# A graph layer's end list written anew, with its sums in another PSUM bank and the first rows' normalization cut into parts

## The chip, the cores and the metric

The kernel runs on one core of a Trainium2 chip. The metric is device microseconds of one execution. Several executions are timed and their median is taken; one more execution is taken with the hardware profiler, and all rows shown here are from that one.

## The reference

A graph layer with 12,500 nodes of 128 features and 200,000 edges, sorted by destination. What is computed, cut to what matters:

```python
h = maximum(layernorm(x), 0)                       # N x 128
score = ((h @ W_Q.T)[dst] * (h @ W_K.T)[src]).sum(-1) / sqrt(128) * exp(-edge_weight)
# of each node the 16 best edges are kept; softmax over them
alpha = w / denom[dst]
agg = segment_sum(alpha[:, None] * (h[src] @ W_msg.T), dst)
out = x + relu(h @ W_self.T + agg)
```

## The kernel before, in words

The edges stand in 1,563 chunks of 128. Fourteen chunks make a group: 112 groups, numbered 0 to 111. The last one, called L in the code, has 9 chunks. A group owns the nodes whose edges begin in it, and it reads one chunk of the next group too, so it works on 15 chunks.

For each chunk GpSimd gathers 128 rows of normalized features from the table `h_tab` in HBM with one indirect DMA (`let_go` and `gather`, L176). VectorE copies the indices first (`ix`, L191). The rows of a group lie in a tile `hs`; there are eight such buffers, so the rows of group 8 go where those of group 0 lay. Groups 0 to 3 (`RAW`) are gathered before the table exists: their raw rows come from the input `x`, and are normalized in place, by one ScalarE activation for each chunk (`normed`, L221). Groups 0 and 1 are normalized in the preparation. Groups 2 and 3 are begun in window 0 (`raw_begun`, one chunk) and finished at the end of windows 1 and 2 (`raw_finished`, 13 chunks in one block).

The work on one group is a pipeline of small stages, each a few instructions:

- `far_of`, `to_edges`, `edges_turned`, `away`, `places`: TensorE and ScalarE build one-hot matrices of which edge belongs to which node and slot. All their matmuls write the one PSUM bank named `a`, and ScalarE empties it.
- `q_to_edges` (L589) spreads the query to edges, in blocks of four chunks; `scores` (L598, VectorE) multiplies it with the gathered rows, one instruction a chunk; `scores_in_slots` (L606).
- `slots_by_node` (L614), `slots_out` (L619, ScalarE), `node_by_slots` (L622): scores are put in 40 slots for each node. These use the PSUM bank `e`.
- `best` (L628 to L640, VectorE): reads bank `e`, finds the 16 best; `sum_of_exps` (L645, ScalarE).
- `kept_to_edges` (L657) brings the marks back to edges, in the bank `x`; `one_over_sum`, `on_edges` (L650 to L670, VectorE), `exps` (L674, ScalarE), `weights` (L678 and L679, VectorE, into `alz`).
- `sums` (L687): 15 accumulating matmuls of weights and rows, each in two passes, into columns 384 to 511 of bank `e`; `sums_out` (L692, ScalarE).
- `sums_turned` (L695), `sums_turned_out` (L699, ScalarE), `products` (L702 and L703), `output` (L707, VectorE), `store`: all in the bank `s`. The last four groups are stored by an indirect DMA of GpSimd (L716).

The instruction order is written by hand. The loop over `i` from -3 to 110 is a window: in it group `i` is scored, group `i-1` is put in slots, `i-2` gets its best, `i-3` its weights and sums, `i-4` its output, while `i+1` and `i+2` are prepared. Each engine executes its part of this list in order. Instructions of different engines on one PSUM bank wait for each other, whichever columns they use. After the loop a second list, written out call by call, brings groups L-5 to L to their ends: this is the end list. One small check of the inputs (`later`, L452 to L470) is executed by VectorE at the end of each early window.

Of the kernel before, what the change touches and what calls it, by code (L numbers as in the profile page):

```python
# [14 lines left out]
AF = mybir.ActivationFunctionType  # L15
OP = mybir.AluOpType
# [4 lines left out]
P = 128  # L21
# [29 lines left out]
PRE = 16  # L51
STEP = 8
WW = STEP * (NJ - 1) + WN
# [23 lines left out]
def gnn_layer(  # L77
# [27 lines left out]
    nc = tc.nc  # L105
# [26 lines left out]
    def bank(tag, bufs):  # L132
        return psum.tile([P, 512], F32, tag=tag, bufs=bufs, name=tag)
# [81 lines left out]
    def normed(rows, n0, n1, rs, sm):  # L215

        if n0 == 0:
            nc.vector.reciprocal(rs, rs)
            nc.vector.scalar_tensor_tensor(sm, sm, -0.5, rs, op0=OP.mult, op1=OP.mult)
        for t in range(n0, n1):  # L220
            nc.scalar.activation(rows[:, t, :], rows[:, t, :], AF.Relu, bias=sm[:, t:t + 1],  # L221
                                 scale=rs[:, t:t + 1])
# [9 lines left out]
    def raw_begun(g):  # L232
        normed(T[g]["hs"], 0, 1, *T[g]["raw"])

    def raw_finished(g):
        normed(T[g]["hs"], 1, own[g], *T[g]["raw"])

    w0 = rows_pool.tile([P, NJ], F32, name="w0")
    zpad = rows_pool.tile([P, D], F32, name="zpad")
# [15 lines left out]
    with tc.tile_pool(name="edges", bufs=1) as ep, ExitStack() as stage:  # L255
# [38 lines left out]
        xs, t = [], 0  # L294
# [208 lines left out]
    with tc.tile_pool(name="win", bufs=2) as win:  # L503
# [79 lines left out]
        def q_to_edges(g, b):  # L583
            j0, j1 = 4 * b, min(4 * b + 4, chunks[g])
            if j0 >= j1:
                return
            T[g]["pq", b] = pq = bank("q", 3)
            for j in range(j0, j1):
                nc.tensor.matmul(pq[:, (j - j0) * P:(j - j0 + 1) * P],  # L589
                                 lhsT=T[g]["to_e"][:, j * P:(j + 1) * P], rhs=T[g]["q"], start=True, stop=True)  # L590

        def scores(g, b):
            if b == 0:
                T[g]["s"] = win.tile([P, NJ], F32, name="s", bufs=4)
            for j in range(4 * b, min(4 * b + 4, chunks[g])):
                c = GC * g + j
                prod = win.tile([P, D], F32, name="prod")
                nc.vector.scalar_tensor_tensor(  # L598
                    prod, rows_of(g, j), dec_all[:, c:c + 1],
                    T[g]["pq", b][:, (j % 4) * P:(j % 4 + 1) * P],  # L600
                    op0=OP.mult, op1=OP.mult, accum_out=T[g]["s"][:, j:j + 1])
# [15 lines left out]
        def slots_out(g):  # L617
            T[g]["eT"] = win.tile([KM + 1, P], F32, name="eT")
            nc.scalar.copy(T[g]["eT"], et[0:KM + 1, PRE:PRE + P])  # L619

        def node_by_slots(g):
            nc.tensor.transpose(et[:, 256:256 + KM + 1], T[g]["eT"], ident[0:KM + 1, 0:KM + 1])  # L622
# [31 lines left out]
        def kept_to_edges(g):  # L654
            T[g]["px"] = px = psum.tile([P, NJ + 1, 64], F32, tag="x", bufs=1, name="x")
            for j in range(chunks[g]):
                nc.tensor.matmul(px[:, j, 0:KM + 3], lhsT=upper(T[g]["to_e"][:, j * P:(j + 1) * P]),  # L657
                                 rhs=upper(T[g]["km"]), start=True, stop=True)
# [17 lines left out]
        def weights(g):  # L676
            n, kept = chunks[g], T[g]["kept"]
            nc.vector.tensor_tensor(kept[:, 0:n], T[g]["up"][:, 0:n], kept[:, 0:n], op=OP.mult)  # L678
            nc.vector.tensor_tensor(alz[g % 2].rearrange("e (j w) -> e j w", w=WW + STEP)[:, 0:n, 0:WN],  # L679
                                    T[g]["ow"][:, 0:n, :], bc(kept[:, 0:n], WN), op=OP.mult)  # L680


        def sums(g, part):
            n = chunks[g]
            half = n // 2
            for j in range(half) if part == 0 else range(half, n):
                nc.tensor.matmul(et[:, 384:384 + P], lhsT=alz[g % 2][:, WW * j + PRE:WW * j + PRE + P],  # L687
                                 rhs=rows_of(g, j), start=(j == 0), stop=(j == n - 1))

        def sums_out(g):  # L690
            T[g]["agn"] = win.tile([P, D], F32, name="agn")
            nc.scalar.activation(T[g]["agn"], et[:, 384:384 + P], AF.Copy, scale=T[g]["rden"])  # L692

        def sums_turned(g):
            nc.tensor.transpose(so[:, 2 * P:3 * P], T[g]["agn"], ident)  # L695
# [24 lines left out]
        def at(g, stage, *args):  # L720
            if 0 <= g < G:
                stage(g, *args)


        for i in range(-3, G - 1):
            at(i + 3, load_nodes)
            if i == 8:
                nc.sync.dma_start(h_tab[N:N + P, :], zpad)
                nc.sync.dma_start(x_end[XT:XT + P, :], zpad)
                nc.sync.dma_start(x_end[0:XT, :], x[N - XT:N, :])  # L730
            def more(k):

                if i in (-1, 0, 1):
                    g = i + 6
                else:
                    g, k = (i + 4, k + 2) if k < 5 else (i + 5, k - 5)
                    if g < 8:
                        return
                if i >= -1 and g < G:
                    let_go(g, k)  # L740

            at(i, q_to_edges, 0)
            at(i - 5, output)
            at(i - 5, store)
            at(i - 3, weights)
            more(0)
            at(i - 4, sums_turned)
            at(i + 1, far_of, 0)
            at(i - 4, sums_turned_out)
            at(i + 1, q_out)  # L750
            at(i, q_to_edges, 1)
            at(i + 1, far_of, 1)
            for b in range(3):
                at(i - 1, slots_by_node, b)
            at(i + 1, far_of, 2)
            more(1)
            at(i - 2, best)
            more(2)
            at(i - 2, sum_of_exps)
            at(i - 1, slots_out)  # L760
            at(i, q_to_edges, 2)
            at(i + 1, far_of, 3)
            at(i + 2, h_turned)
            at(i, scores, 0)
            more(3)
            at(i + 1, to_edges)
            at(i + 2, h_turned_out)
            at(i - 2, kept_to_edges)
            at(i - 1, node_by_slots)
            at(i + 1, edges_turned)  # L770
            at(i - 3, sums, 0)
            at(i, scores, 1)
            more(4)
            at(i + 1, away, 0)
            at(i, q_to_edges, 3)
            at(i - 2, one_over_sum)
            at(i + 1, away, 1)
            at(i - 3, sums, 1)
            at(i, scores, 2)
            at(i - 2, on_edges)  # L780
            more(5)
            at(i + 1, away, 2)
            at(i - 3, sums_out)
            at(i - 4, products)
            at(i - 2, exps)
            at(i + 1, places)
            at(i, scores, 3)
            at(i, scores_in_slots)
            if i == 0:
                raw_stats(2)  # L790
                raw_stats(3)
                raw_begun(2)
                raw_begun(3)
            if i in (1, 2):
                raw_finished(i + 1)
            more(6)
            at(i + 2, q_made)
            if i > 0 and later:
                later.pop(0)()
# [5 lines left out]
        def turned(g):  # L805
            sums_turned(g)
            sums_turned_out(g)

        def all_sums(g):
            sums(g, 0)  # L810
            sums(g, 1)
            sums_out(g)

        def to_rows(g):
            products(g)
            output(g)
            store(g)

        def all_slots(g):
            for b in range(3):  # L820
                slots_by_node(g, b)

        def to_nodes(g):
            all_slots(g)
            slots_out(g)
            node_by_slots(g)

        def kept_on_edges(g):
            one_over_sum(g)
            on_edges(g)  # L830
            exps(g)
# [4 lines left out]
        weights(L - 3)  # L836
        turned(L - 4)
        all_slots(L - 1)
        slots_out(L - 1)
        best(L - 2)  # L840
        sum_of_exps(L - 2)
        q_to_edges(L, 1)
        node_by_slots(L - 1)
        to_rows(L - 4)
        all_sums(L - 3)
        kept_to_edges(L - 2)
        best(L - 1)
        sum_of_exps(L - 1)
        scores(L, 0)
        kept_on_edges(L - 2)  # L850
        turned(L - 3)
        kept_to_edges(L - 1)
        scores(L, 1)
        weights(L - 2)
        all_sums(L - 2)
        to_rows(L - 3)
        for b in range(2, blocks):
            q_to_edges(L, b)
            scores(L, b)
        scores_in_slots(L)  # L860
        to_nodes(L)
        kept_on_edges(L - 1)
        turned(L - 2)
        best(L)
        sum_of_exps(L)
        weights(L - 1)
        kept_to_edges(L)
        all_sums(L - 1)
        to_rows(L - 2)
        kept_on_edges(L)  # L870
        turned(L - 1)
        weights(L)
        all_sums(L)
        to_rows(L - 1)
        turned(L)
# [184 lines left out]
```

## Time and profile before

| | us |
|---|---|
| timed executions | 2051.35, 2051.93, 2052.34 |
| median | 2051.93 |
| profiled execution, its time | 2049.57 |
| profiled execution, its span | 2047.8 |
| gathers, 1507 of them, mean | 0.955 |
| start of the last gather of rows | 1995.29 |
| end of the last `output` (L707) | 2033.39 |

The span runs from the first to the last recorded instruction; 1.77 us of the time lie outside it. TensorE's share of busy time is 77%, GpSimd's 74%, VectorE's 63% and ScalarE's 50%, as averages over stages that have different limits.

### The profile page before, as it was taken

The numbers are of one execution on the slowest core, as the hardware profiler recorded it, in microseconds if no ns is written. First come the engines' busy times: TensorE is split into PE (matmuls) and PEld (weight loads), VectorE is DVE, ScalarE is ACT, GpSimd is POOL, SyncE is SP. The second block draws the span as 40 slices with busy tenths as digits, with TensorE's granted clock in tenths as the row PEclk, the third lists the DMA queues.
The fourth block names the chain that finished last, engine by engine and source line by source line (L and its number), as shares of the span: only waits on it lengthen the run. The fifth ranks groups of instructions, "written<-read, shape, count | busy, mean of one in ns | idle before, by whom it ended". The sixth has DMA issues, their size and how long they took to land. (4 is left out here: it accounts for less than half of the span.)

```text
span 2047.8 us, 42217 instructions
## 1 busy us (share of the span) xinstructions
PE 1581.4 (77%) x13800; PEld 1304.9 (64%) x13801; DVE 1281.2 (63%) x7001; ACT 1026.3 (50%) x2198; POOL 1508.7 (74%) x1580
## 2 busy tenths in 40 slices
PE   0368899987787878878888778787888888777784
PEld 0257777766666666666666666666666666666663
DVE  7567877766666666666666666566666666666553
ACT  6666566544444444444444445444444445444440
POOL 6777777777777777777777777777777777777770
PEclk9969999998998999999899999899999989989887
DMA  9521222222222222222222222222222222222220
GB/s 246 154 57 52 76 68 68 66 65 65 66 64 65 65 66 66 63 64 66 66 65 65 65 65 66 65 66 65 64 63 65 65 65 66 66 65 66 63 59 7
DMA packets 101472, 143.46 MB, mean 70 GB/s; under 512 B 31063, under 2 KB 74327, under 8 KB 100480
## 3 DMA queue, kind: packets, MB, share of 16 engines
q0 software_dynamic: 50144, 102.74, 19.2%
q1 hardware_dynamic: 51102, 37.99, 6.7%
q8 instruction: 108, 1.77, 0.4%
q14 instruction: 118, 0.97, 0.2%
HBM read 126.79 MB, written 14.40 MB: 69 GB/s over the span
## 5 line engine op out<-in xcount | busy, mean ns | idle before, releaser
L176 POOL DMA_INDIRECT hs<-h_tab,ix x1507 | 1439.9, 955 | 464.9 <-issue 303.5
L598 DVE SCALAR_TENSOR_TENSOR prod<-hs,dec_all,q 128x128 f32<-128x128 f32 x1674 | 508.0, 343 | 298.2 <-DMA hs<-h_tab,ix 260.0
L551 ACT ACTIVATE far<-a,minus 128x512 bf16<-128x512 f32 (+1 forms) x447 | 294.5, 659 | 534.9 <-PE a L549 527.7
L589 PE MATMUL q<-q,to_e 128*128 128x128 f32 x3348 | 515.3, 301 | 0.0
L589 PEld LDWEIGHTS q<-q,to_e 128*128 128x128 f32 x3348 | 484.7, 214 | 34.1 <-DVE prod L598 13.5
L687 PE MATMUL e<-hs,alz 128*128 128x128 f32 x3348 | 436.7, 284 | 4.6 <-DVE alz L679 4.6
L687 PEld LDWEIGHTS e<-hs,alz 128*128 128x128 f32 x3348 | 394.9, 193 | 32.0 <-issue 19.2
L574 ACT ACTIVATE aw<-a 128x400 bf16<-128x400 f32 x336 | 169.4, 504 | 312.7 <-PE a L572 312.7
L628 DVE TENSOR_SCALAR ell<-slots,e 128x40 f32<-128x40 f32 x112 | 28.4, 254 | 369.8 <-PE e L614 319.0
L695 PE MATMUL s<-ident,agn 128*128 128x128 f32 x112 | 38.2, 341 | 266.6 <-DVE kept L678 265.4
L549 PE MATMUL a<-rel,ident 112*128 112x512 bf16 (+1 forms) x447 | 196.1, 439 | 14.8 <-ACT far L551 14.8
L556 ACT ACTIVATE to_e<-far 128x1920 f32<-128x1920 bf16 x112 | 201.4, 1799 | 3.5
L695 PEld LDWEIGHTS s<-ident,agn 128*128 128x128 f32 x112 | 16.9, 151 | 282.7 <-issue 280.4
L614 PE MATMUL e<-opo,sl 128*41 128x40 f32 x3348 | 189.8, 230 | 0.9 <-DVE rden L650 0.9
L614 PEld LDWEIGHTS e<-opo,sl 128*41 128x41 f32 x3348 | 176.1, 144 | 13.2 <-DVE sl L606 1.0
L598 DVE DVE_READ_ACCUMULATOR prod<-hs,dec_all,q 128x1 f32 x1674 | 136.8, 82 | 0.0
L578 ACT ACTIVATE opo<-aw 128x1200 f32<-128x1200 bf16 x112 | 134.2, 1199 | 0.1
L191 DVE COPY ix<-idx_all 128x2 int32<-128x2 int32 x754 | 132.8, 191 | 0.0
L572 PE MATMUL a<-minus_at,pdT 32*128 32x400 bf16 x336 | 115.0, 342 | 18.0 <-ACT pdT L565 7.6
L657 PE MATMUL x<-km,to_e 128*128 128x43 bf16 x1674 | 61.4, 184 | 70.9 <-DVE km L640 66.0
L657 PEld LDWEIGHTS <-to_e 128*128 128x128 bf16 x1674 | 50.1, 97 | 102.3 <-DVE km L640 96.8
L606 DVE TENSOR_TENSOR sl<-opo,s 128x600 f32<-128x600 f32 x112 | 87.5, 782 | 3.9
(174 smaller groups left out, 1646.5 us busy)
## 6 DMA issues: line engine op xcount, KB each, us to landing
hs<-h_tab,ix POOLq DMA_INDIRECT x1507
h_r<-h_tab SPq DMA_DIRECT2D x112, 64.0 KB
x_t<-in_x_dram SPq DMA_DIRECT2D x108, 64.0 KB
out_dram<-o SPq DMA_DIRECT2D x108, 64.0 KB
xg<-in_x_dram SPq DMA_DIRECT2D x2, 1400.0 KB
h_tab<-xg SPq DMA_DIRECT2D x2, 1400.0 KB
xg<-in_x_dram SPq DMA_DIRECT2D x1, 1120.0 KB
h_tab<-xg SPq DMA_DIRECT2D x1, 1120.0 KB
```

What stands on the lines that cost most here:

```text
L176: nc.gpsimd.indirect_dma_start(out=T[g]["hs"][:, j, :], out_offset=None, in_=table[0:N, :], in_offset=bass.IndirectOffsetOnAxis(ap=index(j ...
L191: nc.vector.tensor_copy(ix[:, j0:j1], idx_all[:, GC * g + j0:GC * g + j1])
L549: nc.tensor.matmul(pr[:, 0:n1 - n0], lhsT=upper(ident[0:RR, g:g + 1]).to_broadcast([RR, P]), rhs=rel[:, n0:n1], start=True, stop=True)
L551: nc.scalar.activation(T[g]["far"][:, n0:n1], pr[:, 0:n1 - n0], AF.Square, bias=minus)
L556: nc.scalar.activation(T[g]["to_e"][:, 0:n], T[g]["far"][:, 0:n], AF.Relu, bias=1.0, scale=-1.0)
L572: nc.tensor.matmul(pr[:, 0:400], lhsT=T[g]["pdT"], rhs=minus_at.rearrange("k w j s -> k (w j s)")[:, n0:n1], start=True, stop=True)
L574: nc.scalar.activation(T[g]["aw"][:, n0:n1], pr[:, 0:400], AF.Square)
L578: nc.scalar.activation(T[g]["opo"].rearrange("e w j s -> e (w j s)"), T[g]["aw"], AF.Relu, bias=1.0, scale=-1.0)
L589: nc.tensor.matmul(pq[:, (j - j0) * P:(j - j0 + 1) * P], lhsT=T[g]["to_e"][:, j * P:(j + 1) * P], rhs=T[g]["q"], start=True, stop=True)
L598: nc.vector.scalar_tensor_tensor(prod, rows_of(g, j), dec_all[:, c:c + 1], T[g]["pq", b][:, (j % 4) * P:(j % 4 + 1) * P], op0=OP.mult, op1 ...
L614: nc.tensor.matmul(et[0:KM + 1, STEP * j:STEP * j + WN], lhsT=sl1[g % 2][:, j, :], rhs=T[g]["ow"][:, j, :], start=False, stop=(j == n - 1))
L687: nc.tensor.matmul(et[:, 384:384 + P], lhsT=alz[g % 2][:, WW * j + PRE:WW * j + PRE + P], rhs=rows_of(g, j), start=(j == 0), stop=(j == n ...
```

## The change

Three things are done. In the end list, the order of the calls is new, and all calls of `sums` write the bank `a` in place of bank `e` (inside the loop they stay in `e`). The normalization of the raw rows of groups 2 and 3 is no longer one block of 13 activations at the end of windows 1 and 2: three parts of three chunks go to ScalarE at three places in the same windows, and the last four chunks go to VectorE, as two `tensor_scalar` instructions each, where the block was.

```diff
-    def raw_finished(g):
-        normed(T[g]["hs"], 1, own[g], *T[g]["raw"])
+    def raw_finished(g, part):
+        rows, (rs, sm) = T[g]["hs"], T[g]["raw"]
+        if part < 3:
+            normed(rows, 1 + 3 * part, 4 + 3 * part, rs, sm)
+            return
+        for t in range(10, own[g]):
+            nc.vector.tensor_scalar(rows[:, t, :], rows[:, t, :], rs[:, t:t + 1], sm[:, t:t + 1],
+                                    op0=OP.mult, op1=OP.add)
+            nc.vector.tensor_scalar(rows[:, t, :], rows[:, t, :], 0.0, None, op0=OP.max)
...
-        def sums(g, part):
+        def sums(g, part, at=None):
             n = chunks[g]
+            if part == 0:
+                T[g]["pa"] = et[:, 384:384 + P] if at is None else at
             half = n // 2
             for j in range(half) if part == 0 else range(half, n):
-                nc.tensor.matmul(et[:, 384:384 + P], lhsT=alz[g % 2][:, WW * j + PRE:WW * j + PRE + P],
+                nc.tensor.matmul(T[g]["pa"], lhsT=alz[g % 2][:, WW * j + PRE:WW * j + PRE + P],
                                  rhs=rows_of(g, j), start=(j == 0), stop=(j == n - 1))
...
-            nc.scalar.activation(T[g]["agn"], et[:, 384:384 + P], AF.Copy, scale=T[g]["rden"])
+            nc.scalar.activation(T[g]["agn"], T[g]["pa"], AF.Copy, scale=T[g]["rden"])
...
+            def raw(part):
+                if i in (1, 2):
+                    raw_finished(i + 1, part)
...
             at(i + 1, far_of, 1)
+            raw(0)
             for b in range(3):
                 at(i - 1, slots_by_node, b)
...
             at(i - 1, slots_out)
+            raw(1)
             at(i, q_to_edges, 2)
             at(i + 1, far_of, 3)
+            raw(2)
             at(i + 2, h_turned)
...
             if i in (1, 2):
-                raw_finished(i + 1)
+                raw_finished(i + 1, 3)
...
         def all_sums(g):
-            sums(g, 0)
+            sums(g, 0, bank("a", 1)[:, 0:P])
             sums(g, 1)
             sums_out(g)
```

The two end lists side by side, from the first line in which they differ. `all_slots` holds `slots_out` now; `blocks` is 3, of four, four and one chunks.

```python
# before                                  # after
all_slots(L-1); slots_out(L-1)            all_slots(L-1)
best(L-2); sum_of_exps(L-2)               best(L-2); sum_of_exps(L-2)
q_to_edges(L, 1)                          q_to_edges(L, 1); q_to_edges(L, 2)
node_by_slots(L-1); to_rows(L-4)          node_by_slots(L-1); to_rows(L-4)
all_sums(L-3)                             kept_to_edges(L-2)
kept_to_edges(L-2)                        all_sums(L-3)
best(L-1); sum_of_exps(L-1)               scores(L, 0)
scores(L, 0)                              kept_on_edges(L-2)
kept_on_edges(L-2)                        best(L-1); sum_of_exps(L-1)
turned(L-3)                               weights(L-2)
kept_to_edges(L-1)                        kept_to_edges(L-1)
scores(L, 1)                              scores(L, 1)
weights(L-2); all_sums(L-2)               turned(L-3); all_sums(L-2)
to_rows(L-3)                              scores(L, 2)
q_to_edges(L, 2); scores(L, 2)            scores_in_slots(L); all_slots(L)
scores_in_slots(L)                        products(L-3); node_by_slots(L)
all_slots(L); slots_out(L)                kept_on_edges(L-1); weights(L-1)
node_by_slots(L); kept_on_edges(L-1)      output(L-3); store(L-3)
turned(L-2); best(L); sum_of_exps(L)      best(L); sum_of_exps(L); turned(L-2)
weights(L-1); kept_to_edges(L)            sums(L-1, 0); kept_to_edges(L)
all_sums(L-1)                             sums(L-1, 1); sums_out(L-1)
to_rows(L-2)                              to_rows(L-2)
kept_on_edges(L); turned(L-1)             kept_on_edges(L); weights(L)
weights(L); all_sums(L)                   turned(L-1); all_sums(L)
to_rows(L-1); turned(L); to_rows(L)       to_rows(L-1); turned(L); to_rows(L)
```

More of the change, by code (lines that the diff above doesn't have):

```diff
@@ L821, in all_slots @@
                 slots_by_node(g, b)
-        def to_nodes(g):
-            all_slots(g)
             slots_out(g)
-            node_by_slots(g)
         def kept_on_edges(g):
@@ L838, in gnn_layer @@
         all_slots(L - 1)
-        slots_out(L - 1)
         best(L - 2)
         sum_of_exps(L - 2)
-        q_to_edges(L, 1)
+        for b in range(1, blocks):
+            q_to_edges(L, b)
         node_by_slots(L - 1)
         to_rows(L - 4)
+        kept_to_edges(L - 2)
         all_sums(L - 3)
-        kept_to_edges(L - 2)
+        scores(L, 0)
+        kept_on_edges(L - 2)
         best(L - 1)
         sum_of_exps(L - 1)
-        scores(L, 0)
-        kept_on_edges(L - 2)
-        turned(L - 3)
+        weights(L - 2)
         kept_to_edges(L - 1)
         scores(L, 1)
-        weights(L - 2)
+        turned(L - 3)
         all_sums(L - 2)
-        to_rows(L - 3)
         for b in range(2, blocks):
-            q_to_edges(L, b)
             scores(L, b)
         scores_in_slots(L)
-        to_nodes(L)
+        all_slots(L)
+        products(L - 3)
+        node_by_slots(L)
         kept_on_edges(L - 1)
-        turned(L - 2)
+        weights(L - 1)
+        output(L - 3)
+        store(L - 3)
         best(L)
         sum_of_exps(L)
-        weights(L - 1)
+        turned(L - 2)
+        pa = bank("a", 1)[:, 0:P]
+        sums(L - 1, 0, pa)
         kept_to_edges(L)
-        all_sums(L - 1)
+        sums(L - 1, 1)
+        sums_out(L - 1)
         to_rows(L - 2)
         kept_on_edges(L)
+        weights(L)
         turned(L - 1)
-        weights(L)
         all_sums(L)
```

## The prediction, written before the changed kernel was run

> **What bounds the kernel now.** The groups of the page come first. GpSimd's gathers are the longest row, and 303.5 of their 464.9 us of idle time are "issue", which is 0.30 us ahead of each gather.
>
> ```profile
> L176 POOL DMA_INDIRECT hs<-h_tab,ix x1507 | 1439.9, 955 | 464.9 <-issue 303.5
> ```
>
> A gather of 0.95 and a pause of 0.30 make 1.25, so 14 make 17.5 us for each group; the timeline shows windows 17.4 apart. The loop ends when the gathers end. Then only three places can move the time: a gather that waits for more than 0.30, a gather that lasts longer, and what comes after the last gather. The view of waits, for GpSimd, answers the first: one wait stands out, 5.7 us, on the index copy of L191.
>
> ```profile
> POOL hs L176 <- DVE ix L191: 18.2, 42, 5.7
> ```
>
> GpSimd's timeline puts it at 165.4, and TensorE's shows what really ended it.
>
> ```profile
> 164.42 0.95 POOL L176 DMA_INDIRECT hs<-h_tab,ix  x1 [0.30 <-issue]
> 171.11 2.60 POOL L176 DMA_INDIRECT hs<-h_tab,ix  x1 [5.75 <-DVE ix L191]
> ...
> 168.52 2.05 PE L687 MATMUL e<-hs,alz 128*128 128x128 f32 x16
> ```
>
> The index copy is at 169.23; the gather still waits. It is the first of group 8, and writes the buffer of group 0, whose sums end at 168.52 + 2.05 = 170.57. Every later gather follows 1.25 or more after the one before it, so the rest of the loop inherits this stall: 5.75 - 0.30 = 5.45 us. It is the most that can be had at this place.
>
> ScalarE's timeline shows why group 0 is late: the raw rows' blocks.
>
> ```profile
> 133.75 5.09 ACT L221 ACTIVATE hs<-hs,smr,rsr 128x128 f32<-128x128 f32 x13
> 138.75 0.67 ACT L551 ACTIVATE far<-a,minus 128x512 bf16<-128x512 f32 x1
> ...
> 152.94 5.09 ACT L221 ACTIVATE hs<-hs,smr,rsr 128x128 f32<-128x128 f32 x13
> 157.94 0.67 ACT L551 ACTIVATE far<-a,minus 128x512 bf16<-128x512 f32 x1
> ```
>
> The L551 behind each block empties bank a, and TensorE stands until then: 2.83 us before its next matmul in one window, 3.57 in the other.
>
> Last, the end. After the last gather starts, at 1995.29, the last output ends at 2033.39, 38.1 us later, for one group and parts of three others. The lines to see:
>
> ```profile
> 1998.28 0.25 DVE L628 TENSOR_SCALAR ell<-slots,e 128x40 f32<-128x40 f32 x1 [3.46 <-ACT agn L692]
> ...
> 2005.71 6.12 PE L687 MATMUL e<-hs,alz 128*128 128x128 f32 x30 [2.05 <-DVE alz L679]
> 2011.93 0.37 ACT L692 ACTIVATE agn<-e,rden 128x128 f32<-128x128 f32 x1 [9.34 <-PE e L687]
> 2024.05 0.29 DVE L707 SCALAR_TENSOR_TENSOR o<-s,x_t 128x128 f32<-128x128 f32 x1 [5.43 <-ACT agn L692]
> ```
>
> L628 needs scores that lay in bank e at 1993.7; it waits for the sums of group 108 in the same bank. Later VectorE and TensorE take turns: TensorE's sums wait for `alz`, VectorE's next step for the sums. And the same 30 matmuls last 3.51 at 1994.33, 6.12 at 2005.71, 4.82 at 2018.68. The stretches of 3.4 us show why:
>
> ```profile
> 1994.00:1997.40 3.40, 3.40 (x32) 3.40 (x32) 0.29 (x1) 0.00 (x0) 1.89 (x2) 1.00 0.32 82
> 2000.80:2004.20 3.40, 0.73 (x15) 0.61 (x15) 3.26 (x18) 0.37 (x2) 0.00 (x0) 0.50 0.00 0
> 2004.20:2007.70 3.50, 1.99 (x9) 2.00 (x10) 1.42 (x8) 0.00 (x0) 0.00 (x0) 0.50 0.00 0
> 2007.70:2011.10 3.40, 3.40 (x18) 3.40 (x17) 0.00 (x0) 0.00 (x0) 0.00 (x0) 0.52 0.00 0
> 2011.10:2014.50 3.40, 2.46 (x32) 2.08 (x30) 1.99 (x10) 0.38 (x2) 1.00 (x1) 1.00 0.00 0
> ```
>
> (The first column after the length is TensorE's busy time; the column before the DMA share is its granted clock.) It falls to half when TensorE has waited.
>
> **Part 1, the raw rows: what comes off.** At 133.75 the next `far` matmul was done at 134.29 + 0.63 = 134.92, so without the block L551 starts at 134.95 and not 138.75: 3.80 less. In the next window the matmul ends at 153.48 + 0.63 = 154.11, against 157.94: again 3.80. Sum 7.60.
>
> **What is put back on ScalarE.** One activation costs 5.09 / 13 = 0.39, a part of three 1.17. Part 0 follows the second `far`; there ScalarE idles 2.35 and 1.86, waiting for L549, so it is hidden, and would cost its 1.17 if L549 came at once. Part 1 follows `slots_out`: in window 1 ScalarE idles 1.20 there, hidden; in window 2 L551 followed at once (144.88), so 1.17. Part 2 stands ahead of `to_edges`, which feeds L565, L574 and the window's end without a gap: 1.17 in both windows. Back: 3.5. Net 7.60 - 3.5 = 4.1.
>
> **On VectorE**, eight instructions a window are added. The trace has no such form. From below: a TENSOR_SCALAR of one element (L650, 0.15). From above: the 128x128 scores (0.34). The nearest is L200 with 128 elements, 2.80 / 14 = 0.20; I take it, so 1.6 a window (1.2 to 2.7). Queued behind it are the window's `later` check, the last index copies (made at 132.2, used by a gather at 163.2) and the next L628, which idled 6.44 and 7.57 for L614. These shrink by the 3.80 gained and still hold 1.6. Without that cover it would be 3.2 in all.
>
> **The clock adds to it.** With TensorE's 2.83 and 3.57 us of idle time gone, the following stretches (0.57 granted in 140 to 144, 0.50 in 160 to 164) may run at full speed. TensorE works from 139.46 to 143.89 on the chain to L551, 4.4 us; at full clock up to 2 less, and the same again after 158.66. So group 0's sums come 4.1 to 8 earlier, and the stall gives at most 5.45.
>
> **Where a rule speaks against it.** The gather started at 151.59, inside L464 on VectorE (151.40 to 153.30, both inputs in SBUF), took 2.53 in place of 0.94. The Trainium skill, SBUF — State Buffer, section "Who interferes with whom", says more: VectorE's `tensor_scalar` between SBUF tiles can take both ports of the pair shared with GpSimd, and GpSimd is then shut out for the whole instruction. By that rule the 16 new instructions could add 16 x 0.20 = 3.2 us to the gathers before group 8: these would be ready at 165.67 + 3.2, and the stall gives only 2.25. By the trace a gather is held only where it starts inside a VectorE instruction: `alz` from 1936.83 to 1937.61 began during a gather that still took 0.94. Each run of eight meets one or two starts: 0.2 to 0.4 us in all. I take 5.0 for part 1 (2.2 to 5.45): the 4.1, with some clock, less the held gathers. The end list then begins 5.0 earlier as a whole.
>
> **Part 2, the end list**, worked on the clock of before, up to the same L619 (ends 1991.78), with TensorE at full clock from 1994.0.
>
> - TensorE: the ten `q` matmuls from 1991.42 (eight took 2.0 at half clock, two more 0.45), transpose and products until 1994.6; L657 (0.45), then the sums of 108: 1995.0 to 1998.5. Before, they ended 0.7 earlier.
> - VectorE: output 1994.9, four scores (0.27 each), `on_edges` of 109 (2.28 from L650 to its next), `best` of 110 (1.97), which no longer waits for the sums: until 2000.4. `weights` of 109: 0.20 + 0.78, `alz` ends 2001.4. Before: 2005.65. Its `exps` waits for L692 on ScalarE, until 1999.1; covered.
> - TensorE: L657 for 110 at 2000.5, sums of 109 from 2001.5, 3.5 at full clock: 2005.0. Before: 2011.83. So 6.8 here, of which 2.6 is clock.
> - VectorE meanwhile: five scores, L606, `on_edges` of 110: until 2005.4. Then a new wait: `exps` of 110 stands on ScalarE behind L692 of 109 and L619 of 111, which waits for L614 (2005.0 to 2006.0). So `weights` of 110 starts at 2006.6, `alz` ends 2007.6. Queued behind it: output of 108 and `best` of 111, until 2009.8.
> - TensorE: products of 108, L622, transpose; the sums of 110 in two halves, 1.64 and 1.87, around L657 of 111 (0.3, at 2009.85): until 2012.0. Products of 109 until 2012.6.
> - VectorE: output of 109 at 2012.65. From here both lists have the same chain. It lasted from 2024.05 to 2033.39, 9.34. So 2022.0, and 2033.39 - 2022.0 = 11.4.
>
> The third and fourth store keep their distance, and the 14.4 from the last output to the span's end stay. No DMA is added.
>
> **What the clock makes of it.** The Trainium skill, TensorE: Matmul & The Clock Gate, section "What's actually happening", has the clock fall after at least one idle stretch of 3.4 us, and rise after a busy one. By that no stretch of the new list is idle, and all stays fast. The trace is stricter: 0.73 of 3.40 busy kept half clock, 1.99 of 3.50 too. In the new list TensorE stands 2.0 us before L657 of 110, and about 1 before the transpose of 109, so the sums of 109 may cost 6.1 (2.6 more) and those of 110 up to 6.4 in place of 3.5 (2.9 more). All slow: 11.4 - 5.5 = 5.9. All fast, the last sums too (18 matmuls, 3.26 before, 18 x 0.117 = 2.1): 12.6. Where the stretches fall is not known; I keep 11.4.
>
> **Sum.** 5.0 + 11.4 = 16.4. The profiled execution took 2049.57 (span 2047.8 and 1.77 around it): 2033.2, span 2031.4. The median of the runs shown is 2.36 above the profiled one: 2051.93 - 16.4 = 2035.5.
>
> **Rivals.**
> - *Held gathers* (0.10): the port costs the whole 3.2. For it: L464's gather. Against: `alz`. Gain 2.2 + 11.4 = 13.6: 2038.3.
> - *Half clock in the end* (0.12): for it, 0.50 with 1.99 of 3.50 busy. Against: less standing still than before. Gain 5.0 + 5.9 = 10.9: 2041.0.
> - *The waits come back one step on* (0.03), in ScalarE's order (`exps` behind L619) and in bank a, so that VectorE and TensorE still take turns and only some 3 of part 1 stays: 2048.9, within 0.2% of before (4.1 us, about what a measurement of this kernel can tell from no change).
> - *Slower* (0.03): each of the 16 new VectorE instructions holds GpSimd as L464 did, 1.59. GpSimd is then ready for group 8 at 165.67 + 25.4 = 191.1, 20.0 after 171.11; less 11.4 at the end it is 8.6 slower: 2060.5. It decides from 16.9 / 16 = 1.05 us for each. Against: only long instructions held one so.
>
> **Numbers.** The main case has 0.72. Its own range follows from the bounds: part 1 from 3.5 to 5.45, the end from 9.5 to 14 (best phase of the clock, and steps that overlap better than I placed them): 2032.5 to 2039. With the two first rivals the range is 2031.5 to 2041.0. Faster 0.94, same 0.03, slower 0.03.
>
> **What would show it.** Right: GpSimd's first gather of group 8 starts near 166, with no idle time over 1.5; L628's 3.46 is gone; the last gather starts near 1990.3; from there to the last output's end 26 to 28 us; the sums of 109 last about 3.5. Wrong: gathers over 1.3 us in 130 to 165 beside the new VectorE rows (held gathers); 6 us for the sums of 109 and 110 (clock); a new wait of VectorE of over 3 us after 1991.

## The result, and the profile after

| | before | after |
|---|---|---|
| median of six executions each | 2050.94 | 2033.22 (2027.74 to 2036.32) |
| ratio, 95% interval | | 0.9913 (0.9897 to 0.9930) |
| profiled execution, time and span | 2049.57, 2047.8 | 2036.32, 2034.5 |
| last gather starts | 1995.29 | 1991.09 |
| last output ends | 2033.39 | 2020.14 |

2035.5 was forecast, 16.4 under the 2051.93 that it was counted from; the medians lie 17.7 apart. The profiled execution of after is the slowest of its six, so the two traces differ by only 13.3 in their spans: 4.20 up to the start of the last gather, and 9.05 in the end, which is counted from there to the end of the last output.

**The loop.** The gathers' row of the page is almost what it was, and in GpSimd's timeline the wait of 5.75 ahead of group 8 (the "stall" below) is 1.25.

```profile
L176 POOL DMA_INDIRECT hs<-h_tab,ix x1507 | 1436.4, 953 | 461.9 <-issue 304.6
```

```profile
166.71 0.94 POOL L176 DMA_INDIRECT hs<-h_tab,ix  x1 [0.30 <-issue]
168.91 1.19 POOL L176 DMA_INDIRECT hs<-h_tab,ix  x1 [1.25 <-PE a L579]
171.97 1.00 POOL L176 DMA_INDIRECT hs<-h_tab,ix  x1 [1.87 <-issue]
173.27 0.94 POOL L176 DMA_INDIRECT hs<-h_tab,ix  x1 [0.30 <-issue]
```

The third line is new to the argument: the second gather of group 8 starts 3.06 after the first, which had waited, and not 1.25. It did so before too (171.11, then 174.17), hidden in a row that read 2.60.

ScalarE's and TensorE's timelines show the raw parts, and what they moved.

```profile
131.88 0.51 PE L579 MATMUL a<-minus_at,pdT 32*128 32x400 bf16 x1 [2.92 <-ACT pdT L572]
138.39 0.69 ACT L558 ACTIVATE far<-a,minus 128x512 bf16<-128x512 f32 x1 [1.12 <-PE a L556]
145.09 1.26 ACT L221 ACTIVATE hs<-hs,smr,rsr 128x128 f32<-128x128 f32 x3
146.26 0.56 ACT L558 ACTIVATE far<-a,minus 128x384 bf16<-128x384 f32 x1
146.72 1.25 ACT L221 ACTIVATE hs<-hs,smr,rsr 128x128 f32<-128x128 f32 x3
147.88 1.79 ACT L563 ACTIVATE to_e<-far 128x1920 f32<-128x1920 bf16 x1
149.72 0.25 ACT L572 CAST pdT<-a 32x128 bf16<-32x128 f32 x1
150.02 0.51 PE L579 MATMUL a<-minus_at,pdT 32*128 32x400 bf16 x1 [2.93 <-ACT pdT L572]
156.28 1.92 PE L596 MATMUL q<-q,to_e 128*128 128x128 f32 x8
156.53 0.69 ACT L558 ACTIVATE far<-a,minus 128x512 bf16<-128x512 f32 x1 [1.12 <-PE a L556]
166.31 2.05 PE L696 MATMUL e<-hs,alz 128*128 128x128 f32 x16
```

The `far` of windows 1, 2 and 3 start at 121.86, 138.39 and 156.53 (before: 120.08, 138.75, 157.94). Window 1 is 16.53 long in place of 18.67, window 2 18.14 in place of 19.19, and from there to the end of group 0's sums it is 11.83 in place of 12.63: 2.14 + 1.05 + 0.80 = 3.99. TensorE's 2.83 and 3.57 us behind the block are gone, but it now waits 2.92 and 2.93 at L579 for `pdT` (1.92 before), since part 2 stands ahead of `to_edges`. So eight `q` matmuls still take 1.92 at 156.28, half clock. Right behind them the clock does rise, where the prediction thought it might. The view by stretches for 160 to 164, before and then after (the first busy time is TensorE's, the granted clock stands ahead of the DMA share):

```profile
160.00:164.00 4.00, 4.00 (x35) 3.77 (x34) 2.02 (x13) 1.24 (x4) 3.09 (x4) 0.50 0.23 56
160.00:164.00 4.00, 3.39 (x37) 2.87 (x37) 3.74 (x27) 2.96 (x6) 2.99 (x4) 1.00 0.33 86
```

From 140 to 144 it is 0.84 in place of 0.57. No raw rows stand in window 3, so its 0.80 is not from ScalarE's order; the thirty matmuls of `slots_by_node` last 1.37 in it in place of 2.32.

VectorE's new rows, and the gathers beside them:

```profile
135.64 0.35 DVE L241 TENSOR_SCALAR hs<-hs,rsr,smr 128x128 f32<-128x128 f32 x1
135.73 0.94 POOL L176 DMA_INDIRECT hs<-h_tab,ix  x1 [0.30 <-issue]
136.03 0.23 DVE L243 TENSOR_SCALAR hs<-hs 128x128 f32<-128x128 f32 x1
136.17 0.56 DVE L241 TENSOR_SCALAR hs<-hs,rsr,smr 128x128 f32<-128x128 f32 x1
...
136.98 0.94 POOL L176 DMA_INDIRECT hs<-h_tab,ix  x1 [0.30 <-DVE hs L241]
...
138.22 3.23 DVE L459 TENSOR_TENSOR dl_n<-pd,w 128x1680 f32<-128x1680 bf16 x1
139.48 2.74 POOL L176 DMA_INDIRECT hs<-h_tab,ix  x1 [0.30 <-issue]
...
142.39 0.25 DVE L635 TENSOR_SCALAR ell<-slots,e 128x40 f32<-128x40 f32 x1 [0.94 <-ACT hs L221]
```

Eight of them last 2.5 us, and the gathers that start beside them take 0.94. It is VectorE that is held, a little: the L241 of 136.17 runs in the last part of the gather of 135.73 and ends at 136.73, 0.06 after it. In the runs e7, e8 and b2, where no gather stands beside these rows, every L241 takes 0.34. The gather that is held (2.74) is again one that starts inside a long check. Of VectorE's idle time ahead of `best` (6.44 and 7.57 before) 0.94 and 1.07 are left: the cover was just enough.

**The end.** The 3.46 wait of `best` of 110 is gone. What stands in the timelines now:

```profile
1998.30 5.14 PE L696 MATMUL a<-hs,alz 128*128 128x128 f32 x30 [0.20 <-DVE alz L686]
2004.88 0.17 DVE L685 TENSOR_TENSOR kept<-up,kept 128x15 f32<-128x15 f32 x1 [2.45 <-ACT up L681]
2010.90 0.29 DVE L716 SCALAR_TENSOR_TENSOR o<-s,x_t 128x128 f32<-128x128 f32 x1 [2.88 <-ACT agn L701]
2013.84 3.01 PE L696 MATMUL a<-hs,alz 128*128 128x128 f32 x18 [2.20 <-DVE alz L686]
```

The new wait of `weights` of 110 is there (2.45), and the sums of 109 take 5.14. The view by stretches has the reason, a clock that fell:

```profile
1994.00:1997.40 3.40, 1.52 (x15) 1.33 (x13) 3.16 (x15) 0.87 (x4) 0.00 (x0) 1.00 0.00 0
1997.40:2000.80 3.40, 3.21 (x27) 3.02 (x28) 3.23 (x18) 0.27 (x1) 0.00 (x0) 0.61 0.00 0
...
2011.00:2014.40 3.40, 0.86 (x6) 0.70 (x7) 2.51 (x10) 0.36 (x2) 1.00 (x1) 1.00 0.05 17
2014.40:2017.90 3.50, 3.30 (x20) 3.01 (x18) 0.10 (x1) 0.37 (x1) 0.00 (x0) 0.61 0.00 0
```

### The profile page after: what moved, and what is told of

Read it like the earlier page. It is cut to its first block, busy times and chain, and to the rows that moved or that the text cites. A ratio compares the mean times of both kernels' runs of the same rounds, so it can differ in the third digit from the quotient of the medians.

```text
span 2034.5 us, 42215 instructions
## 1 busy us (share of the span) xinstructions
PE 1580.1 (78%) x13800; PEld 1303.9 (64%) x13801; DVE 1284.9 (63%) x7017; ACT 1021.7 (50%) x2190; POOL 1505.6 (74%) x1580
## 5 line engine op out<-in xcount | busy, mean ns | idle before, releaser
L696 PE MATMUL e<-hs,alz 128*128 128x128 f32 x3240 | 419.1, 282 | 0.0
L696 PEld LDWEIGHTS e<-hs,alz 128*128 128x128 f32 x3240 | 377.9, 192 | 26.9 <-issue 19.2
L621 PE MATMUL e<-opo,sl 128*41 128x40 f32 x3348 | 194.0, 233 | 0.0
L579 PE MATMUL a<-minus_at,pdT 32*128 32x400 bf16 x336 | 115.4, 343 | 19.3 <-ACT pdT L572 9.6
```

What stands on the lines that cost most here:

```text
L579: nc.tensor.matmul(pr[:, 0:400], lhsT=T[g]["pdT"], rhs=minus_at.rearrange("k w j s -> k (w j s)")[:, n0:n1], start=True, stop=True)
L621: nc.tensor.matmul(et[0:KM + 1, STEP * j:STEP * j + WN], lhsT=sl1[g % 2][:, j, :], rhs=T[g]["ow"][:, j, :], start=False, stop=(j == n - 1))
L696: nc.tensor.matmul(T[g]["pa"], lhsT=alz[g % 2][:, WW * j + PRE:WW * j + PRE + P], rhs=rows_of(g, j), start=(j == 0), stop=(j == n - 1))
```

## The experiments

e1 to e4 ran on a chip where before takes 2054.48. The others ran on three chips where every kernel takes half as long again (before: 3159.23 for e5 to e8, 3123.89 for b1, e9 and e10, 3155.35 for b2): a gather lasts 0.96 to 0.97 there in the mean, but a group takes 26.8 to 27.2 us, not 17.6. Why is not shown by these traces. In the view of waits of e10 (total, times, longest) engines wait for something that the view calls "remote", and the gathers wait for the sums:

```profile
ACT aw L582 <- remote: 596.4, 98, 6.2
POOL hs L176 <- PE e L697: 579.0, 98, 6.0
```

On those chips the stall ahead of group 8 is 24 to 28 us whatever the raw rows do, so they say nothing on part 1. Their last gather starts some 51 us ahead of `best` of 109, so the end list shows there undisturbed by the gathers, and from `best` of 109 on its rows can be compared. The changed kernel itself was not run on these chips; e5, e6 and e10 have its list, e7 and e9 have it with added matmuls. In the table, "old list" is the end list of before and "new list" that of after, and the times are in us, by the timelines:

| kernel | loop paced by | `best` of 109 to the last output's end | to the last store's start |
|---|---|---|---|
| before | gathers | 41.57 | 42.94 |
| e1, part 1 alone (old list) | gathers | 43.89 | 45.23 |
| after, and e3, the same again | gathers | 31.68, 31.25 | 32.87, 32.59 |
| e2, part 2 alone (new list) | gathers | 31.53 | 32.77 |
| e4, new list, bank `e` | gathers | 30.92 | 32.26 |
| e5, new list, raw rows on ScalarE | other | 27.60 | 28.95 |
| e10, new list, raw rows left out | other | 28.94 | 30.28 |
| e9, new list with added matmuls | other | 27.58 | 28.92 |
| e8, output behind weights | other | 25.81 | 27.17 |
| b1, list anew | other | 23.05 | 26.81 |
| b2, list anew, outputs earlier | other | 23.69 | 24.18 |

**e1, part 1 alone.** The whole end list of before, and its sums:

```diff
-            sums(g, 0, bank("a", 1)[:, 0:P])
+            sums(g, 0)
```

> Only the raw rows' part of the change; the end list and the sums' bank as before. Theory (the stall ahead of group 8's gathers is what part 1 shortens, and the trace of after shows it fall from 5.45 to 0.95 us): gain 4.5, about 2046.4, last gather 4.5 earlier, the end from the last gather to the last output unchanged at 38. Rival (the 2.2 us by which group 8 began earlier is all; the rest of the 4.2 at the last gather is chance in the pace of the gathers): gain 2.2, about 2048.7. Rival (VectorE's eight new instructions a window hold gathers): gathers over 1.3 us beside L241 and L243, gain under 2.2.

Measured: 2049.41, ratio 0.9975 (0.9966 to 0.9984), so 5.07 faster (3.3 to 7.0). Its GpSimd never waits for group 0 (the third line is the first gather of group 8):

```profile
166.39 1.39 POOL L176 DMA_INDIRECT hs<-h_tab,ix  x1 [0.30 <-PE a L579]
168.09 1.58 POOL L176 DMA_INDIRECT hs<-h_tab,ix  x1 [0.30 <-issue]
169.97 0.94 POOL L176 DMA_INDIRECT hs<-h_tab,ix  x1 [0.30 <-issue]
171.22 0.95 POOL L176 DMA_INDIRECT hs<-h_tab,ix  x1 [0.30 <-issue]
```

From the first gather out of `h_tab` to the third gather of group 8 it takes 77.66 us. With the old block this was 83.71 (before) and 83.05 (part 2 alone); with the parts 79.27 (after), 80.15 (after once more) and 82.18 (bank `e`). Against the mean of the two old ones, part 1 gives 1.2 to 5.7, 3.6 in the mean of four, and it differs between executions of the same loop code. After's own profile gains 4.4 against that of before; its gathers began 2.29 later (94.00 against 91.71), and on the 1,448 after group 8 it was 2.05 quicker. The rival of 2.2 mistook the late start for the gain.

**e2, part 2 alone.**

```diff
-            raw(0)
...
-            raw(1)
...
-            raw(2)
...
-                raw_finished(i + 1, 3)
+                raw_finished(i + 1)
```

`raw_finished` itself is that of before again.

> Only the end list with its sums in bank a; the raw rows as before. Theory (the end saves what the profile of after shows, 9.05): about 2041.9, last gather where it was before, 29 us from it to the last output. Rival (the profiled run of after was a poor one in the end, the median end saves the 11.4 forecast or more, up to 13.2, which is the whole gain of the medians, 17.7, less 4.5): 2037.7 to 2039.5, with 25 to 27 us from the last gather to the last output.

Measured: 2042.97, ratio 0.9941 (0.9928 to 0.9955): 11.5 faster, though its end is 28.96 from the last gather, as in after. Each expectation held in one half: the new end in this profile is the 29 of the profile of after, and the gain of the medians is the larger number. One reading is that the old end is usually longer than the 38.1 of the profile of before. The one other profile with the old list, e1's, has 41.27: its sums there last 3.53, 6.32, 6.55 and 3.68, against 3.51, 6.12, 4.82 and 3.26. It is not shown for the medians: an end can be read from a profiled execution alone, and that of e2 was the slowest of its five, 3.0 over their median, with the latest first gather of all (95.54). The parts add up: 5.07 + 11.51 = 16.58, and 17.38 for both on this chip.

**e3, after once more**, unchanged.

> The changed kernel once more, for a second profile and a steadier time. Theory (half-clock stretches fall otherwise in every execution and make the end 26 to 29 us long): 2033.2 in the median, spread of 5 us or more, sums of 109 between 3.5 and 6.1 with the granted clock of their stretch 1.00 to 0.50. Rival (the end is the same in every execution): 29.0 from the last gather to the last output again, sums of 109 5.1 again.

Measured: 2037.10 (2035.13 to 2039.15), ratio 0.9916 (0.9903 to 0.9930). The end is 28.67 from the last gather, the sums of 109 4.95. So the rival is nearer: three profiles of the new end (after, e2, e3) lie within 0.4, though in e4 below, with the same order, the sums of 109 ran at full clock. What does differ between them is the start: the first gather out of `h_tab` begins between 91.56 and 95.54.

**e4, sums back in bank e, order kept.**

```diff
-            sums(g, 0, bank("a", 1)[:, 0:P])
+            sums(g, 0)
...
-        sums(L - 1, 0, pa)
+        sums(L - 1, 0)
```

> The changed kernel with the end list's sums back in bank e, order unchanged. Theory (the order carries the gain, the bank little: best of 110 would wait 0.65 for the sums of 108 to leave e, the slots of 111 0.54 for those of 109, the sums of 110 0.2 for best of 111): 1.4 slower than the changed kernel, about 2034.6. Rival (the bank is what took away the 3.46 us wait of L628): 3.5 slower, about 2036.7. Rival (ScalarE has slack enough, bank e is as good): no difference.

Measured: 2039.27, ratio 0.9926 (0.9913 to 0.9940), 2.2 over after, with intervals that overlap. Its `best` of 110 waits 0.57, not 3.46, and its list is 30.92. The clock fell elsewhere in it: its sums of 109 ran at full clock (3.62 against 4.95 to 5.14), its last sums more at half (3.87 against 3.01 to 3.20). Without these two rows its list is 23.43, and 23.10 to 23.53 in after, e2 and e3. So the order carries the gain, and what the bank adds does not stand out from those 0.4. The 2.2 of the medians may come from the stall ahead of group 8, which was 3.86 in its profile, in code that is the same as after's.

**e5, raw rows all on ScalarE; e6 and e10, left out.**

```diff
+        normed(rows, 1 + 3 * part, 4 + 3 * part if part < 3 else own[g], rs, sm)   # e5, whole body
...
+        return                                                                     # e6, e10, first line
```

> The changed kernel with the raw rows' last four chunks on ScalarE at the window's end, in the place of VectorE's eight instructions. Theory (ScalarE idles 1.12 us ahead of the next window's first far, so four activations of 0.39, 1.56, delay it 0.44 in each of two windows): stall ahead of group 8 0.9 longer, time 0.9 over the changed kernel, inside the scatter. Rival (VectorE's part carries the gain of part 1): 3.1 slower. Rival (VectorE's instructions hold gathers or the window): faster than the changed kernel by up to 2.

> The norming of rows 1 to 13 of groups 2 and 3 is left out, on both engines. Theory (all that part 1 can still give is the stall left ahead of group 8, 0.95 and 1.67 in two profiles of the changed kernel): no idle time over 0.4 ahead of group 8, time 1 to 2 under the changed kernel. Rival (the raw rows still cost the 2.4 us a window of VectorE or the 3.8 of ScalarE): 4 or more under it.

> The kernel without the norming of rows 1 to 13 of groups 2 and 3 once more, on a chip where the gathers set the pace of the loop. Theory (part 1 has taken all but the rest of the stall): no idle time over 0.4 ahead of group 8, 1 to 2 faster than the changed kernel. Rival (the parts still cost their 2.4 us of VectorE or 3.8 of ScalarE a window): 4 or more faster.

Measured: 3139.78, 0.9940 (0.9927 to 0.9954); 3137.90, 0.9931 (0.9917 to 0.9944); 3101.39, 0.9921 (0.9907 to 0.9936). All three ran where the stall ahead of group 8 is 24 to 28 us, so none of the theories was tried. What VectorE's share of part 1 is worth stays open.

**e7 and e9, clock kept up in the end.** `warm(n)` issues n matmuls of `ident` into a `q` bank that nothing reads.

```diff
+        warm(6)
         kept_to_edges(L - 1)
...
         turned(L - 1)
+        warm(8)
         all_sums(L)
```

> The changed kernel with idle-time matmuls of TensorE into a bank that nothing reads: six ahead of the kept slots of 110 (1.4 us at full clock, in an idle time of 1.88) and eight ahead of the last sums (1.9 in 2.20). Theory (half clock after idle time is what lengthens the sums): sums of 109 3.5 in place of 5.0, sums of 111 2.1 in place of 3.0 to 3.2, the end 26.2 in place of 28.8, 2.5 faster than the changed kernel. Rival (the added matmuls stand in the way, or the stretches fall as they fall): the end 28.5 to 30, no gain.

> The kernel with idle-time matmuls once more (six ahead of the kept slots of 110, eight ahead of the last sums), on a chip where the gathers set the pace of the loop. On the chip where the loop was far slower the changed list took 25.6 us from the output of 107 to the last output at full clock, with the added matmuls and without. Theory (half clock is what makes it 28.4 in the profiles of the changed kernel here): 25.6 to 26.3, sums of 109 3.6, last sums 2.2 to 2.3, 2.5 faster than the changed kernel, ratio 0.990 to 0.9905. Rival (the rows are longer for another reason, as the gathers' landing): 28 or more.

Measured: 3139.54, 0.9938 (0.9925 to 0.9952); 3105.80, 0.9940 (0.9926 to 0.9955). No gain in time there. But e9 and e10 have the same list and chip, and the rows of their last sums tell the clock apart. The stretches are now 3.41 us long and laid on the moments at which the granted clock changes. Without the added matmuls (e10), timeline and stretches:

```profile
3078.12 3.64 PE L697 MATMUL a<-hs,alz 128*128 128x128 f32 x18 [2.20 <-DVE alz L687]
```

```profile
3074.19:3077.60 3.41, 1.20 (x9) 0.84 (x8) 2.14 (x10) 0.73 (x3) 1.00 (x1) 1.00 0.05 17
3077.60:3081.02 3.42, 2.90 (x13) 2.90 (x14) 0.47 (x1) 0.00 (x0) 0.00 (x0) 0.50 0.00 0
```

With them (e9; 1.7 of the 2.87 busy us are theirs):

```profile
3071.53 1.95 PE L848 MATMUL q<-ident 128*128 128x128 f32 x16
3073.89 2.27 PE L696 MATMUL a<-hs,alz 128*128 128x128 f32 x18 [0.41 <-DVE alz L686]
```

```profile
3069.85:3073.26 3.41, 2.87 (x26) 2.71 (x25) 2.07 (x9) 0.73 (x3) 1.00 (x1) 1.00 0.05 17
3073.26:3076.68 3.42, 2.94 (x24) 2.55 (x23) 0.54 (x2) 0.37 (x1) 0.00 (x0) 1.00 0.00 0
```

1.37 of the 3.64 of the same 18 matmuls is half clock, behind 2.2 us of standing still. It does not always come: in e5 and e6, with the same list and the same 2.20, the last sums took 2.27 all the same, and on that chip the added matmuls of e7 changed nothing (27.58 against 27.60). The difference is where the wait falls. In e10 1.68 us of it lie in one stretch. In e5 it is divided over two, 0.90 and 1.30, and the clock stays:

```profile
3115.18:3118.59 3.41, 1.97 (x16) 1.62 (x15) 1.50 (x8) 0.73 (x3) 1.00 (x1) 1.00 0.00 0
3118.59:3122.01 3.42, 2.12 (x19) 2.12 (x20) 1.11 (x3) 0.00 (x0) 0.00 (x0) 1.00 0.05 17
```

The sums of 109 fit this. The stretch ahead of theirs has 1.51 busy in after and 1.53 in e2 and e3, and 0.50 follows; in e4 it has 1.97, and 1.00 follows. A limit for other places is not to be had from it: in the loop of e9 a stretch with 2.28 busy (2673.90 to 2677.31) was followed by 0.50.

**e8, the output of 109 behind the weights of 111.**

```diff
-        to_rows(L - 2)
+        products(L - 2)
         kept_on_edges(L)
         weights(L)
+        output(L - 2)
+        store(L - 2)
```

> The changed kernel with the output of group 109 behind the weights of 111 on VectorE, where it had made VectorE wait 2.88 us for TensorE's products ahead of the last group's kept slots. Theory (that wait is on the path of the last sums): alz of 111 2.4 earlier, the last sums start 2.0 to 2.4 earlier (TensorE is busy with the sums of 110 until then), the end 26 to 27, 2.0 to 3.0 faster than the changed kernel. Rival (TensorE is the bound there, or the bank of the products holds the transpose): under 1.

Measured: 3137.82, ratio 0.9932 (0.9918 to 0.9945); list 25.81 against 27.58 (e7) and 27.60 (e5) on the same chip, 1.8 shorter, a little under the 2.0 to 3.0 expected. The last sums follow without a wait:

```profile
3115.76 0.53 DVE L686 TENSOR_TENSOR alz<-opo,kept 128x360 f32<-128x360 f32 x1
3116.21 0.28 DVE L716 SCALAR_TENSOR_TENSOR o<-s,x_t 128x128 f32<-128x128 f32 x1
3116.64 0.30 PE L704 MATMUL s<-ident,agn 128*128 128x128 f32 x1 [1.24 <-DVE o L716]
3116.78 2.17 PE L696 MATMUL a<-hs,alz 128*128 128x128 f32 x18
```

**b1 and b2, the list anew.** In both, raw part 2 stands behind the first `aw`, sums and products use the `q` banks, and the last two outputs are written into `agn`. The core of b1's calls, in order:

```python
best(L - 2); kept_to_edges(L - 2); scores(L, 0); output(L - 4); sums(L - 3)
on_edges(L - 2); exps(L - 2); weights(L - 2); sums_out(L - 3)
sums(L - 2, 0, place("q")); best(L - 1); kept_to_edges(L - 1)
scores(L, 1); scores(L, 2); scores_in_slots(L); sums(L - 2, 1)
on_edges(L - 1); exps(L - 1); all_slots(L); weights(L - 1); products(L - 3)
best(L); output(L - 3); sums(L - 1, 0, place("q")); kept_to_edges(L)
sums(L - 1, 1); on_edges(L); exps(L); weights(L); products(L - 2); output(L - 2)
sums(L); products(L - 1); output(L - 1); products(L); output(L)
```

> The changed kernel with another end list and with the raw rows' part 2 moved behind the first `aw` on ScalarE. In the list: each weighting stands right behind its kept slots, ahead of the next `best`; exps stand ahead of the sums' eviction on ScalarE; the slots of 111 and the kept slots stand between the halves of the sums; the sums and products take the q banks, free by then; outputs stand where VectorE waits. Theory (VectorE and TensorE are made to wait by the order; in the profile of after VectorE waits 2.45 and 2.88 us and TensorE 1.88 and 2.20): sums of 109 start 2.5 earlier, the last sums 5 to 6 earlier, the end from the last gather 22 to 24 in place of 28.8; the raw part 2 takes up to 1 off the stall ahead of group 8; in all 5 to 7.5 faster than the changed kernel, 2047 less 17 less 6 over the same before, a ratio of 0.988 to 0.989. Rival (the clock takes it back, since TensorE then stands as long elsewhere): the end 25 to 27, ratio 0.990. Rival (TensorE is the bound of the list): under 2.

Measured: 3100.21, ratio 0.9916 (0.9902 to 0.9931). The list is 23.05, 4.5 shorter, but the last store starts 26.81 after `best` of 109, 2.1 earlier. GpSimd's timeline:

```profile
3074.44 1.01 POOL L726 DMA_INDIRECT out_dram<-o,idxo  x1 [66.82 <-DVE up L671]
3077.50 1.00 POOL L726 DMA_INDIRECT out_dram<-o,idxo  x1 [2.05 <-DVE o L717]
3080.49 0.98 POOL L726 DMA_INDIRECT out_dram<-agn,idxo  x1 [1.99 <-issue]
3084.37 0.98 POOL L726 DMA_INDIRECT out_dram<-agn,idxo  x1 [2.90 <-DVEq L914]
```

The four stores follow each other by 3.0 or more (the last by 3.88, with a wait that ends at an instruction behind the list, L914, and is not explained here), and the outputs of 109 to 111 now come closer together than that.

In b2 `output(L - 3)`, then `products(L - 2)`, stand ahead of `best(L)`, `output(L - 2)` behind it, and `products(L - 1)` between the halves of `sums(L)`.

> The end list of the last kernel with the outputs of 108 and 109 before and after `best` of 111, and the products of 110 between the halves of the last sums, so that GpSimd's four stores, each about 3.0 us after the one before it (1.0 and 1.99 of issue), no longer set the end. In the last kernel the list took 23.05 us from `best` of 109 to the last output (27.6 in the changed kernel at full clock), but the last store began 26.8 after `best` of 109 (28.95). Theory (GpSimd's stores had become the bound): the last store begins 24.0 to 24.8 after `best` of 109, and the store of 111 at most 1.3 after its output. On a chip whose loop the gathers pace: 4 to 6 faster than the changed kernel, ratio 0.988 to 0.9895. Rival (the last store waits for something else): 26 or more from `best` of 109 to the last store, ratio 0.990 to 0.9915.

Measured: 3130.95, ratio 0.9918 (0.9905 to 0.9932). The last store starts 24.18 after `best` of 109 and 0.49 after its output's end (3116.18 + 0.29):

```profile
3116.96 0.98 POOL L726 DMA_INDIRECT out_dram<-agn,idxo  x1 [1.98 <-DVE agn L717]
```

So the stores had become the bound, and 4.8 us of the changed list (28.95) are gone there. On a chip paced by the gathers this version was not run, and on these chips its ratio lies among those of the other variants (0.9916 to 0.9940): that it beats the changed kernel in time is not shown.

## Why the prediction was right, and where it was not

- *The bound, and where the time can go* held: with the gathers' row almost unchanged, the gain came out at the stall ahead of group 8 and after the last gather. Of the signs that were named, the stall under 1.5 (1.25), the end of L628's wait and the last gather (1991.09 for 1990.3) came; the end of 26 to 28 us (29.05) and sums of 109 of 3.5 (5.14) did not. That both halves match so closely in the medians (5.0 and 5.07, 11.4 and 11.5) is in part luck, as the next points show.
- *Part 1, 5.0.* Part 1 alone measured 5.07. The 4.1 from ScalarE's order looks close to the 3.99 in the trace, but only 3.19 of that came in windows 1 and 2, where the raw rows stand. The other 0.80 came in window 3, where the clock rose as the step "the clock adds to it" had it (1.00 for 0.50 in 160 to 164). That step was mis-sized: it allowed up to 2 in each of two windows, but part of TensorE's idle time did not go, it moved to L579 behind raw part 2 (2.92 and 2.93 for 1.92). The cap of 5.45 failed, in the other direction. When the first gather of group 8 waits, the next one starts 3.06 after it in place of 1.25, so no wait at all there is worth 5.45 + 1.81 = 7.3; the profile of part 1 alone reached 5.7.
- *VectorE's 0.20 an instruction* was 0.31 (2.5 for eight), inside its bounds, and covered, with 0.94 to spare. *Held gathers*: by the Trainium skill, SBUF — State Buffer, section "Who interferes with whom", VectorE's `tensor_scalar` between SBUF tiles could shut GpSimd out; by the same section the one that issues first gets the pair, and the other is blocked. Here gathers beside the new ones took 0.94, as the prediction read from the trace, and what it missed is the other side: two of the four L241 in each window took 0.46 to 0.56 beside a gather, 0.34 without one.
- *The end, 11.4.* Part 2 alone measured 11.5, but not by the sum's steps. The waits came as written: `best` of 110 no longer waits, `weights` of 110 waits for `exps` (2.45), and output 109 to the last output's end is 9.24 (9.34). From the last gather the new end is 28.7 to 29.05, though, and not 26.7. Two terms make up the difference. The sums of 109 took 4.95 to 5.14 against 3.5, which is the clock. And the list began 0.8 to 0.9 later against the gathers than placed: `best` of 109 starts 2.57 to 2.63 ahead of the last gather, 3.47 in before; e1, with the old list, has 2.63 too, so this is not the new order's. (The ten `q` matmuls that follow took 2.50, 1.38 at full clock in e5.) What offsets both is the old end: its 38.1 was read from one execution, and it is 41.3 in another. Of the 5.5 of the rival with half clock 1.6 came, in the sums of 109; those of 110 ran at full clock (1.73 and 2.03).
- *The rule of the clock* (the Trainium skill, TensorE: Matmul & The Clock Gate, "What's actually happening") asks for an idle stretch. Stretches of after with 1.52 and 0.86 us busy of 3.40 were followed by 0.61; that the trace is stricter was right, and keeping the 11.4 in spite of it was the error. What the prediction said of the phase, that it is not known where the stretches fall, is what e5 and e10 show.
- *Waits come back* and *slower* did not come true: the gain did not shrink to some 3, and gathers beside the new rows were not held. Some waits did stay in the new list (2.45 and 2.88 on VectorE), and e8's list was 1.8 shorter without one of them.

## What to carry to other kernels

An end that is read from one execution may be off by 3 us where TensorE's clock falls in it (38.1 and 41.3 here); ask which rows are longer than the same rows elsewhere, before a list is compared with it. When a block is cut in parts, look for the copy that each part now stands ahead of: here TensorE's wait moved to it. And after each gain in an end list look at the next serial resource: here VectorE's wait for an output, then GpSimd's stores, 3.0 us apart.

## What the runs showed of the hardware

- The first gather of group 8, the first to use a buffer again, is followed by the next one only 3.06 later when it had to wait (171.11 and 174.17 in before, 168.91 and 171.97 in after, 174.26 and 177.33 in e2); in e1, where it did not wait, 1.25 later. Gathers that wait do not all do this. In e8 one that had waited 6.10 for the sums is followed after 1.25, so the cause stays open:

```profile
341.13 0.94 POOL L176 DMA_INDIRECT hs<-h_tab,ix  x1 [6.10 <-PE e L696]
342.38 0.94 POOL L176 DMA_INDIRECT hs<-h_tab,ix  x1 [0.30 <-issue]
```

- A 128x128 `tensor_scalar` of VectorE with two pointer scalars (L241) took 0.34 with no gather beside it (all eight in e7, e8 and b2). Where it ran in the last part of a gather, it ended some 0.05 after it and took up to 0.56 (after, e1, e3, e4). The gathers beside these rows kept their 0.94 to 0.95, but for one of 1.13 in e4 that had begun ahead of them.
- In the end list, a stretch of 3.41 us in which TensorE was busy for 1.20 to 1.53 us was followed by the half clock, and one with 1.97 or 2.12 was not (after, e2 to e5, e10). The same list met both, since its waits fall otherwise against these stretches in each execution.
- An indirect store of GpSimd starts 2.96 to 3.06 after the one before it at the earliest, with 1.0 busy.
- Chips differ: the same program took a median of 2051 to 2054 in some of these runs and of 3124 to 3159 on three other chips, though a gather lasts 0.95 to 0.96 and 0.96 to 0.97. The cause stays open.
